# Sign matrices, operand sums and row maxima in a two-layer adjacency kernel: three regroupings

## The chip, the cores and the metric

The kernel runs on one core of one Trainium2 chip. The time is the device time of one execution in microseconds (us), from the first instruction of the program to the last. A core has a matrix engine (TensorE, "PE" in the profile, with its weight loads apart as "PEld"), a vector engine (VectorE, "DVE"), a scalar engine (ScalarE, "ACT"), a general engine (GpSimd, "POOL") and a queue engine (SyncE, "SP"), each with its own list of instructions that it works off in order. Data reach the on-chip memory by DMA transfers, which SyncE, ScalarE or GpSimd issue. The results of TensorE land in PSUM banks, and ScalarE or VectorE takes them from there ("eviction").

## The reference

Two graph layers over 4096 nodes of 512 features, with a dense matrix `adj` of 4096 x 4096. The part that matters, shortened:

```python
# layer 0
bw = sign(w0)
ba = maximum(sign(x), 0)
x  = layernorm(x + relu(adj @ (ba @ bw.T)))
# layer 1
node_att = softmax(x @ node_w, axis=0)
h = x @ edge_w
e = where(adj > 0, h @ h.T, -9e15)
att = node_att * softmax(e, axis=1)
x = layernorm(x + (adj * att) @ (x @ w1) + bias)
```

So layer 0 multiplies a 0/1 matrix by a sign matrix, and then `adj` by the result. Layer 1 needs h, the square matrix `e` with the maximum of each of its rows, and a second product with a 4096 x 4096 matrix.

## The kernel before

The nodes are cut into 32 blocks of 128 (`P`), and into 8 groups of 512 (`W`, `NG = 8`); `BG` = 4 blocks make a group, `KD` = 4 pieces of 128 make up the 512 features, `HG` = 4 pairs of groups (g and g + 4) make up the nodes. TensorE sets the pace nearly everywhere, so the code around it is about what the other engines do and when. Most of the order is found by a scheduler from the data each instruction needs and the order in which the code is written; inside a `tc.manual_schedule(engines=...)` block the named engines take their instructions in written order.

**The sign product and the first two rows of blocks** (lines 165 to 255). `whole(g)` makes the product of the signs for the nodes of group g. It loads the group of x (transposed, 1 MB). Two blocks of nodes are put in one operand: VectorE computes "b > 0, times 2048" into `over` (L186 or L211), and then "a > 0, plus over" into `ba` (L187 or L212). TensorE multiplies `ba` by the weight signs `bw` (L214) into two banks `pw`. Three operations take the two results apart: ScalarE writes `us`, which is rounded so that only the part times 2048 stays (L220), VectorE subtracts it for the first block of `xw` (L222), ScalarE scales it for the second (L223). In group 0, VectorE also makes the weight signs themselves, in two operations for each of four pieces (L204, L206), between those on x. TensorE has nothing to do until the first are there, and is kept busy with products of zeros (`zeros`, L200).

While these products run, two rows of blocks of layer 0's big product (`early`, blocks 0 and 16) are already worked on: `halves(g)` loads four 128 x 128 pieces of `adj` for each of them, and cuts each number into a high part (ScalarE, L236) and the rest (VectorE, L237); `follow(g, ...)` multiplies both parts by `xw` (L246, L247) and adds in the banks `accs`. The loop runs `whole(g + 1)`, `follow(g)`, `halves(g + 1)`. This stage is not in written order: the scheduler mixes the three. Buffers: x and w0 share three (`stream`), the pieces of `adj` share four (`rows`), `hi` and `lo` have two each (`sp`), `ba` has two.

**The other thirty rows of blocks** (to line 383) do the same with 1 MB pieces of `adj` (L363, L365, L373, L374), followed by a layer norm, transposes (L333) and combinations that go out to memory. VectorE and ScalarE are in written order there. `scr` is a buffer of the layer norm. Beside it, `premask` loads parts of `adj`, turns them into masks on VectorE (L281), and stores them through GpSimd's queue (L282).

**h** (lines 386 to 426) is computed by Strassen-Winograd's seven products in place of eight (`seven`). For each pair of groups, four combinations of x are needed as right operands: t1, t2 and t4 on VectorE (L417, L419, L420), t3 on GpSimd (L418). `seven` runs its products in the order 0, 5, 4, 6, 1, 3, 2, each for q = 0 and 1, so there are 14 steps for a pair; t2 serves product 5, t1 product 4, t3 product 6 and t4 product 3. After each step `between_h` may put a `premask` in. The results are added to h on VectorE (L116, L122, L123, L131, L135) or copied by ScalarE (L113, L127).

**`panel(A)`** (from line 765) is called once for each of the eight groups of nodes, in the second half of layer 1. It holds the negated row maxima of the group in `nm`, 128 x 4, and needs them along the free axis and equal on all partitions. For each of four columns TensorE multiplies the column, broadcast to 128 x 128, by the identity (L772); ScalarE copies the bank (L783). The products with `L1065` around it are the attention's.

Of the kernel before, what the change touches and what calls it, by code (L numbers as in the profile page):

```python
# [22 lines left out]
TWO = 2.0**11  # L23
SHIFT = 1.5 * 2.0**34
SPLIT = 6, 4, 3
WARM = 12
# [3 lines left out]
def kernel(  # L30
# [27 lines left out]
    rows = ctx.enter_context(tc.tile_pool(name="rows", bufs=4))  # L58
    small = ctx.enter_context(tc.tile_pool(name="small", bufs=2))
    dram = ctx.enter_context(tc.tile_pool(name="dram", bufs=1, space=bass.MemoryType.DRAM))  # L60
    ps_mm = ctx.enter_context(tc.tile_pool(name="ps_mm", bufs=6, space=bass.MemoryType.PSUM))
# [4 lines left out]
    eps = const.tile([P, 1], F32, name="eps")  # L66
# [92 lines left out]
    with (  # L159
# [14 lines left out]

        us = wp.tile([P, BG // 2, D], F32, name="us", tag="ends")

        def whole(g):

            xt = stream.tile([P, KD, W], F32, name="xt", tag="stream")
            ba = wp.tile([P, KD, W // 2], F32R, name="ba", tag="quarter", bufs=2)  # L180
            pws = [ps_mm.tile([P, D], F32, name="pw", tag="mm") for j in range(BG // 2)]
            order = [(k, j) for j in range(BG // 2) for k in range(KD)]

            def signs(k, over):
                a, b = xt[:, k, : W // 2], xt[:, k, W // 2 :]
                nc.vector.tensor_scalar(over, b, 0.0, TWO, ALU.is_gt, ALU.mult)  # L186
                nc.vector.scalar_tensor_tensor(ba[:, k, :], a, 0.0, over, ALU.is_gt, ALU.add)  # L187

            if g == 0:

                pos = sp.tile([P, KD, D], BF16, name="pos", tag="lo")
                over = sp.tile([P, KD, W // 2], F32, name="over0", tag="hi")
                for k in range(KD):
                    nc.sync.dma_start(w0[:, k, :], w0_t[ts(k, P), :])
                    nc.scalar.dma_start(xt[:, k, :], x_t[ts(k, P), ts(g, W)])
                idle = ps_mm.tile([P, D], F32, name="idle", tag="mm")

                def zeros(n):
                    for _ in range(n):
                        nc.tensor.matmul(idle, warm[:, :P], warm, start=True, stop=True)  # L200

                zeros(WARM)
                for k in range(KD):
                    nc.vector.tensor_scalar(pos[:, k, :], w0[:, k, :], 0.0, None, ALU.is_gt)  # L204
                    signs(k, over[:, k, :])
                    nc.vector.scalar_tensor_tensor(bw[:, k, :], w0[:, k, :], 0.0, pos[:, k, :], ALU.is_lt, ALU.subtract)  # L206
                order = [(k, j) for k in range(KD) for j in range(BG // 2)]
            else:
                nc.sync.dma_start(xt, x_t[:, ts(g, W)].rearrange("(k p) n -> p k n", p=P))
                over = sp.tile([P, KD, W // 2], F32, name="over0", tag="hi")  # L210
                nc.vector.tensor_scalar(over, xt[:, :, W // 2 :], 0.0, TWO, ALU.is_gt, ALU.mult)  # L211
                nc.vector.scalar_tensor_tensor(ba, xt[:, :, : W // 2], 0.0, over, ALU.is_gt, ALU.add)  # L212
            for k, j in order:
                nc.tensor.matmul(pws[j], ba[:, k, ts(j, P)], bw[:, k, :], start=(k == 0), stop=(k == KD - 1))  # L214
                if g == 0 and j == BG // 2 - 1:
                    zeros(3 if k < KD - 1 else 5)
                if k == KD - 1:

                    u = us[:, j, :]
                    nc.scalar.activation(u, pws[j], AF.Identity, bias=shift[:, 0:1])  # L220
                    b = g * BG + j
                    nc.vector.scalar_tensor_tensor(xw[:, b, :], u, SHIFT, pws[j], ALU.subtract, ALU.subtract)  # L222
                    nc.scalar.activation(xw[:, b + BG // 2, :], u, AF.Identity, bias=shift[:, 1:2], scale=-1.0 / TWO)  # L223


        early = [0, HB]
        accs = []

        def halves(g):

            hi = sp.tile([P, QC, P], F32R, name="hi", tag="hi")
            lo = sp.tile([P, QC, P], F32R, name="lo", tag="lo")
            for n, b in enumerate(early):
                a = rows.tile([P, BG, P], F32, name="a0", tag="rows")
                nc.sync.dma_start(a, adj_t[b, :, ts(g, BG), :])
                nc.scalar.copy(hi[:, ts(n, BG), :], a)  # L236
                nc.vector.tensor_sub(lo[:, ts(n, BG), :], a, hi[:, ts(n, BG), :].bitcast(F32))  # L237
            return hi, lo

        def follow(g, hi, lo):  # L240
            if g == 0:
                accs.extend(ps_tr.tile([P, D], F32, name="acc0", tag="tr") for _ in early)
            for n in range(2):
                for c in range(BG):
                    kb = g * BG + c
                    nc.tensor.matmul(accs[n], hi[:, n * BG + c, :], xw[:, kb, :], start=(kb == 0), stop=False)  # L246
                    nc.tensor.matmul(accs[n], lo[:, n * BG + c, :], xw[:, kb, :], start=False, stop=(kb == NB - 1))  # L247

        whole(0)
        parts = halves(0)  # L250
        for g in range(NG):
            if g + 1 < NG:
                whole(g + 1)
            follow(g, *parts)
            if g + 1 < NG:
                parts = halves(g + 1)

        nw_b = wp.tile([P, D], F32, name="nw_b")
        nc.sync.dma_start(nw_b, bass.AP(tensor=node_w.tensor, offset=node_w.offset, ap=[[0, P], [1, D]]))
# [31 lines left out]
        def rest(n, b, xb, acc, before):  # L291

            mv = small.tile([P, 1, nc.vector.BN_AGGR_DIM], F32, name="mv")
            stats = small.tile([P, nc.vector.BN_STATS_DIM], F32, name="stats")
            rstd = small.tile([P, 1], F32, name="rstd")
            scr = wp.tile([P, D], F32, name="scr")
            nc.vector.scalar_tensor_tensor(xb, acc, 0.0, xb, ALU.max, ALU.add)
            nc.vector.bn_stats(stats, xb)
            nc.vector.bn_aggr(mv[:, 0, :], stats)
            yield  # L300
            nc.scalar.activation(rstd, mv[:, :, 1], AF.Sqrt, bias=eps)
            nc.vector.reciprocal(rstd, rstd)
            nc.vector.tensor_scalar(xb, xb, mv[:, 0, 0:1], rstd[:, 0:1], ALU.subtract, ALU.mult)
            nc.vector.tensor_tensor_reduce(
                scr, xb, nw_b, 1.0, 0.0, ALU.mult, ALU.add, accum_out=node_s[:, b : b + 1]
            )
            yield
            nc.vector.tensor_add(scr, xb, bias_b)
            nc.gpsimd.dma_start(x1_d[ts(b, P), :], scr)
            yield  # L310
            if n % 2:
                left(n // 2, before, xb)
            yield
            transpose_rows(b, xb)
# [88 lines left out]
        for _ in range(4):  # L403
            premask(nc.sync, 0, 3)
        count = [0]

        def between_h(q, n):
            count[0] += q is None
            if q is None and count[0] > 6 and count[0] % 5 % 2 == 0:
                premask(nc.sync, 0, 3)  # L410

        for g in range(HG):
            r11, r12 = (x1T[:, :HK, ts(c, W)] for c in (g, g + HG))
            r21, r22 = (x1T[:, HK:, ts(c, W)] for c in (g, g + HG))
            t1, t2 = (sp.tile([P, HK, W], F32, name="t12", tag="hi") for _ in range(2))
            t3, t4 = (sp.tile([P, HK, W], F32, name="t34", tag="lo") for _ in range(2))
            nc.vector.tensor_sub(t1, r12, r11)  # L417
            nc.gpsimd.tensor_sub(t3, r22, r12)  # L418
            nc.vector.tensor_sub(t2, r22, t1)  # L419
            nc.vector.tensor_sub(t4, r21, t2)  # L420
            right_h = r11, r21, r22, t4, t1, t2, t3
            seven(
                lambda m, q: [left_h[m][:, k, ts(q, P)] for k in range(HK)],
                lambda m: [right_h[m][:, k, :] for k in range(HK)],
                [[hT[:, q + f, ts(c, W)] for f in (0, HK) for c in (g, g + HG)] for q in range(2)],
                between_h,
            )
# [337 lines left out]
    def panel(A):  # L765
# [4 lines left out]
        for i in range(BG):  # L770

            nc.tensor.matmul(  # L772
                pt[:, ts(i, P)],
                nm[:, i : i + 1].to_broadcast([P, P]),
                ident,
                start=(i == 0),
                stop=True,
                skip_group_check=i > 0,
            )
        if A % HG:  # L780
# [659 lines left out]
```

## Time and profile before

| | |
|---|---|
| time, three runs | 1941.57 us median (1939.22 to 1943.59) |
| span of the profiled execution | 1940.4 us |
| TensorE busy | 1918.7 us (99%) |
| VectorE busy | 1389.6 us (72%) |
| ScalarE busy | 1022.4 us (53%) |
| GpSimd busy | 299.5 us (15%) |
| moved by DMA | 517.11 MB, mean 267 GB/s |
| weight-sign products L214 | 64, 16.9 us of TensorE |
| early products L246 and L247 | 128, 49.8 us |
| panel products L772 | 64 records, 8.0 us |
| GpSimd's t3, L418 | 4 of 2.34 to 3.20 us |

A line of the timeline is: start in us from the beginning of the span, length in us, engine, source line, operation, output <- inputs by the program's names, partitions x elements and type, count. In brackets is the idle time of the engine just before it, and what ended that idle time. [...] what one costs TensorE is the distance between two starts. A line of the list of waits is: engine and line, what it waited for, us in total, how often, the longest. A line of the windows is: the stretch in us, its length, the busy time of each engine with its number of instructions, the granted TensorE clock, the DMA engines' busy share, GB/s.

### The profile page before, as it was taken

The numbers are of one execution on the slowest core, as the hardware profiler recorded it, in microseconds if no ns is written. First come the engines' busy times: TensorE is split into PE (matmuls) and PEld (weight loads), VectorE is DVE, ScalarE is ACT, GpSimd is POOL, SyncE is SP. The second block draws the span as 40 slices with busy tenths as digits, with TensorE's granted clock in tenths as the row PEclk, the third lists the DMA queues.
The fourth block names the chain that finished last, engine by engine and source line by source line (L and its number), as shares of the span: only waits on it lengthen the run. The fifth ranks groups of instructions, "written<-read, shape, count | busy, mean of one in ns | idle before, by whom it ended". The sixth has DMA issues, their size and how long they took to land.

```text
span 1940.4 us, 20257 instructions
## 1 busy us (share of the span) xinstructions
PE 1918.7 (99%) x6742; PEld 1203.0 (62%) x6742; DVE 1389.6 (72%) x2062; ACT 1022.4 (53%) x1614; POOL 299.5 (15%) x424
## 2 busy tenths in 40 slices
PE   9999999999999999999999999999999999999998
PEld 6888888888644445454555444456666666666655
DVE  7766676676774566567566796687879987798737
ACT  5433333333202567566667566546766576757731
POOL 0122222222341111011112111111111101111100
PEclk9999999999999999999999999999999999999999
DMA  9888888888475478577769998787778787887831
GB/s 311 296 325 310 293 324 308 323 306 293 147 274 213 166 253 320 183 279 254 274 249 336 330 336 296 259 284 248 260 268 290 262 278 254 294 274 265 274 108 44
DMA packets 171751, 517.11 MB, mean 267 GB/s; under 512 B 15872, under 2 KB 41216, under 8 KB 163968
## 3 DMA queue, kind: packets, MB, share of 16 engines
q1 hardware_dynamic: 89472, 226.39, 35.0%
q0 software_dynamic: 66912, 247.49, 34.2%
q10 hardware_dynamic: 15264, 41.95, 5.9%
q8 instruction: 53, 0.87, 0.2%
q14 instruction: 50, 0.41, 0.1%
HBM read 389.94 MB, written 125.83 MB: 266 GB/s over the span
## 4 chain that ended last, share of the span: by engine, by line
PE 76%; DVE 10%; issue 6%; DMA 6%; ACT 1%; POOL 1%; POOLq 0%; DVEq 0%; SPq 0%; ACTq 0%
PE bank L1065 25%; PE seven L702 12%; PE acc L374 11%; PE acc L373 11%; PE pe L633 4%; PE seven L101 4%; PE po L1192 3%; PE pt L603 2%; DMA s_d<-slot 2%; DMA slot<-s_d 2%; DVE lent L835 1%; PE acc L246 1%; PE pw L214 1%; PE pt L333 1%; DVE over L1128 1%
## 5 line engine op out<-in xcount | busy, mean ns | idle before, releaser
L1065 PE MATMUL bank<-lent,lop 128*128 128x512 f32 (+1 forms) x1292 | 424.6, 479 | 0.7 <-issue 0.7
L373 PE MATMUL acc<-xw,hi 128*128 128x512 f32 x960 | 376.4, 392 | 0.0
L374 PE MATMUL acc<-xw,lo 128*128 128x512 f32 x960 | 374.2, 390 | 0.0
L1065 PE MATMUL bank<-slot,lop 128*128 128x512 f32 (+1 forms) x896 | 347.0, 535 | 0.3 <-DVE slot L850 0.3
L1065 PEld LDWEIGHTS bank<-lent,lop 128*128 128x128 f32 x1292 | 245.2, 190 | 155.0 <-issue 133.6
L1065 PEld LDWEIGHTS bank<-slot,lop 128*128 128x128 f32 x896 | 170.0, 190 | 153.4 <-issue 142.3
L363 ACT CAST hi<-at 128x1024 fp32r<-128x1024 f32 x120 | 126.4, 1054 | 203.3 <-PE acc L373 148.4
L365 DVE TENSOR_TENSOR lo<-at,hi 128x1024 fp32r<-128x1024 f32 x120 | 146.9, 1224 | 85.3 <-ACT hi L363 85.3
L374 PEld LDWEIGHTS acc<-xw,lo 128*128 128x128 f32 x960 | 180.3, 188 | 37.0 <-DVE lo L365 0.3
L373 PEld LDWEIGHTS acc<-xw,hi 128*128 128x128 f32 x960 | 180.3, 188 | 36.7
L1074 ACT COPY over<-bank 128x512 f32<-128x512 f32 x200 | 114.9, 581 | 121.3 <-PE bank L1065 109.9
L633 PE MATMUL pe<-hT 128*128 128x512 f32 (+3 forms) x384 | 132.1, 486 | 0.0
L574 ACT ACTIVATE line<-line,nmax_c 128x512 f32<-128x512 f32 x160 | 114.8, 724 | 20.9 <-DVE nmax_c L565 20.8
L565 DVE CUSTOM_DVE_ANT_0 line<-lent,slot 128x512 f32<-128x512 bf16 x144 | 93.1, 689 | 45.2 <-ACT slot L643 22.4
L829 ACT ACTIVATE slot<-slot 128x2048 f32<-128x2048 f32 x40 | 76.5, 1913 | 73.8 <-DMA slot<-in_adj_t_dram 64.7
L823 DVE CUSTOM_DVE_ANT_1 slot<-slot,line 128x2048 f32<-128x2048 f32 x36 | 82.4, 2288 | 32.2 <-DMA slot<-s_d 31.7
L633 PEld LDWEIGHTS pe<-hT 128*128 128x128 f32 x384 | 64.6, 191 | 41.4 <-issue 33.8
L702 PE MATMUL seven<-hT 128*128 128x512 f32 x192 | 89.8, 593 | 0.0
L826 ACT ACTIVATE slot<-slot 128x2048 f32<-128x2048 f32 x36 | 68.9, 1913 | 33.5 <-DVE slot L823 32.5
L1037 ACT COPY bank<-over 128x512 f32<-128x512 f32 x144 | 84.8, 596 | 2.9 <-DVE left L957 0.2
L603 PEld LDWEIGHTS pt<-ident,lent 128*128 128x128 f32 x412 | 51.1, 141 | 55.1 <-issue 40.0
L604 ACT COPY slot<-pt 128x512 f32<-128x512 f32 (+3 forms) x126 | 69.5, 555 | 27.8 <-PE pt L603 24.0
(260 smaller groups left out, 2864.9 us busy)
## 6 DMA issues: line engine op xcount, KB each, us to landing
at<-in_adj_t_dram SPq DMA_DIRECT2D x60, 1024.0 KB, 6.9
slot<-in_adj_t_dram POOLq DMA_DIRECT2D x42, 1024.0 KB, 6.7
lop<-lop_d SPq DMA_DIRECT2D x79, 512.0 KB, 4.7
slot<-s_d POOLq DMA_DIRECT2D x36, 1024.0 KB, 7.5
s_d<-slot POOLq DMA_DIRECT2D x33, 1024.0 KB, 6.9
lent<-s_d POOLq DMA_DIRECT2D x28, 1024.0 KB, 7.9
lop<-lop_d SPq DMA_DIRECT2D x99, 256.0 KB, 4.4
lent<-in_adj_dram SPq DMA_DIRECT2D x48, 512.0 KB, 4.9
```

Source lines behind the costliest of these rows:

```text
L363: nc.scalar.copy(hi, aq)
L365: nc.vector.tensor_sub(lo, aq, hi.bitcast(F32))
L373: nc.tensor.matmul(acc, hi[:, c, :], xw[:, kb, :], start=(kb == 0), stop=False)
L374: nc.tensor.matmul(acc, lo[:, c, :], xw[:, kb, :], start=False, stop=(kb == NB - 1))
L565: nc.vector.tensor_tensor_reduce(line, mask, src, -1.0, HUGE, ALU.add, ALU.min, accum_out=nmax_c[:, b, c : c + 1])
L574: nc.scalar.activation(line, line, AF.Exp, bias=nmax_c[:, b, c : c + 1], scale=-1.0, accum_out=sum_c[:, b, c : c + 1])
L603: nc.tensor.transpose(pt[:, j, :], src[:, ts(j, P)], ident)
L633: nc.tensor.matmul(pe[:, lo * P :], hT[:, k, ts(A * BG + i, P)], hT[:, k, (B * BG + lo) * P : (B + 1) * W], start=(k == 0), stop=(k == KD ...
L702: nc.tensor.matmul(ps, left[m][:, k, q, :], right[m][:, k, :], start=(first and k == 0), stop=(k == KD // 2 - 1), skip_group_check=not first,)
L1037: nc.scalar.copy(self.bank[:, : self.w], self.to())
L1065: nc.tensor.matmul(ps, lop[:, k, :], rop[:, k, :], start=start, stop=(k == K - 1), skip_group_check=True)
L1074: nc.scalar.copy(self.to(), self.bank[:, : self.w])
```

## The change

There are three edits, which don't touch each other.

**The first stage** is rewritten. The weight signs come from ScalarE, one `Sign` with scale -1 for each piece, and a `Sign` on a small tile ahead of them has the function's table loaded early. Of x's group 0, the columns for j = 0 (of both halves) are loaded first, by ScalarE's queue, and those for j = 1 after w0, by SyncE's; the signs of group 0 are made in pieces of 128 columns. `whole` is called for each j, `halves` becomes `split(g, n)` for each of the two early rows, `follow` is called for each n. Loads of x are issued one group further ahead, the signs of x are made one group further ahead, and VectorE, ScalarE and TensorE take all of this in written order. `over` is bf16 and shares a buffer with `scr` in place of one with `hi`.

**h's right combinations** go to VectorE altogether, and those of a pair of groups are made during the products of the pair before, after steps 8, 10 and 13 of its 14.

**`panel`** spreads the row maxima with TensorE's transpose mode: the same operands, with `is_transpose=True`.

```diff
-            if g == 0:
-                pos = sp.tile([P, KD, D], BF16, name="pos", tag="lo")
-                over = sp.tile([P, KD, W // 2], F32, name="over0", tag="hi")
...
-                for k in range(KD):
-                    nc.vector.tensor_scalar(pos[:, k, :], w0[:, k, :], 0.0, None, ALU.is_gt)
-                    signs(k, over[:, k, :])
-                    nc.vector.scalar_tensor_tensor(bw[:, k, :], w0[:, k, :], 0.0, pos[:, k, :], ALU.is_lt, ALU.subtract)
...
+        def signs_x(g):
+            xt = xts.pop(g)
+            ba = wp.tile([P, KD, W // 2], F32R, name="ba", tag="quarter", bufs=2)
+            over = wp.tile([P, KD, W // 2], BF16, name="over0", tag="scr")
...
+            for j in range(BG // 2):
+                for k in range(KD):
+                    if not j:
+                        nc.scalar.activation(bw[:, k, :], w0[:, k, :], AF.Sign, scale=-1.0)
+                    a, b = (xt[:, k, h][:, ts(j, P)] for h in halves)
+                    o = over[:, k, ts(j, P)]
+                    nc.vector.tensor_scalar(o, b, 0.0, TWO, ALU.is_gt, ALU.mult)
+                    nc.vector.scalar_tensor_tensor(ba[:, k, ts(j, P)], a, 0.0, o, ALU.is_gt, ALU.add)
...
+        def whole(g, j):
+            pw = ps_mm.tile([P, D], F32, name="pw", tag="mm")
+            for k in range(KD):
+                nc.tensor.matmul(pw, rights_s[g][:, k, ts(j, P)], bw[:, k, :], start=(k == 0), stop=(k == KD - 1))
+                if g == 0 and (not j or k == KD - 1):
+                    zeros(2 if not j else 4)
...
+        def follow(g, n):
+            hi, lo = split_a[g]
+            for c in (0, 2, 1, 3):
...
+        with tc.manual_schedule(
+            engines={mybir.EngineType.DVE, mybir.EngineType.Activation, mybir.EngineType.PE}
+        ):
+            load_x(0)
...
+            for k in range(KD):
+                nc.sync.dma_start(w0[:, k, :], w0_t[ts(k, P), :])
+                nc.scalar.dma_start(first_x[k][0][:, 0], first_x[k][1][:, 0])
+            for k in range(KD):
+                nc.sync.dma_start(first_x[k][0][:, 1], first_x[k][1][:, 1])
...
+            zeros(WARM)
+            load_a(0, 0)
+            load_x(1)
+            load_a(0, 1)
+            signs_x(0)
+            whole(0, 0)
+            split(0, 0)
+            whole(0, 1)
+            signs_x(1)
+            split(0, 1)
+            for g in range(NG):
+                follow(g, 0)
+                if g + 1 < NG:
+                    for n in range(2):
+                        load_a(g + 1, n)
+                    if g + 2 < NG:
+                        load_x(g + 2)
+                    split(g + 1, 0)
+                    if g:
+                        split(g + 1, 1)
+                        if g + 2 < NG:
+                            signs_x(g + 2)
+                    for j in range(2):
+                        whole(g + 1, j)
+                    if not g:
+                        signs_x(g + 2)
+                        split(g + 1, 1)
+                follow(g, 1)
...
-            nc.gpsimd.tensor_sub(t3, r22, r12)
...
+            nc.vector.tensor_sub(t1, r12, r11)
+            nc.vector.tensor_sub(t2, r22, t1)
+            yield
...
+            nc.vector.tensor_sub(t3, r22, r12)
+            yield
+            nc.vector.tensor_sub(t4, r21, t2)
...
+        ahead_h = deque(p for g in range(1, HG) for p in [rights_h(g)] * 3)
+        for _ in rights_h(0):
+            pass
...
+            if q is None and count[0] % 14 in (8, 10, 13) and ahead_h:
+                next(ahead_h.popleft())
...
                 start=(i == 0),
                 stop=True,
+                is_transpose=True,
                 skip_group_check=i > 0,
```

More of the change, by code (lines that the diff above doesn't have):

```diff
@@ L175 @@
         us = wp.tile([P, BG // 2, D], F32, name="us", tag="ends")
-        def whole(g):
-            xt = stream.tile([P, KD, W], F32, name="xt", tag="stream")
-            ba = wp.tile([P, KD, W // 2], F32R, name="ba", tag="quarter", bufs=2)
[L181 to L187, printed above, removed]
-            if g == 0:
-                pos = sp.tile([P, KD, D], BF16, name="pos", tag="lo")
-                over = sp.tile([P, KD, W // 2], F32, name="over0", tag="hi")
-                for k in range(KD):
[L194 to L202, printed above, removed]
-                for k in range(KD):
-                    nc.vector.tensor_scalar(pos[:, k, :], w0[:, k, :], 0.0, None, ALU.is_gt)
-                    signs(k, over[:, k, :])
-                    nc.vector.scalar_tensor_tensor(bw[:, k, :], w0[:, k, :], 0.0, pos[:, k, :], ALU.is_lt, ALU.subtract)
[L207 to L223, printed above, removed]
@@ L226 @@
[L226 to L238, printed above, removed]
@@ L240, in follow @@
[L240 to L256, printed above, removed]
+        early = [0, HB]
+        accs, xts, rights_s, split_a = [], {}, {}, {}
+        halves = [slice(h * (W // 2), (h + 1) * (W // 2)) for h in range(2)]
+        def load_x(g):
+            xts[g] = stream.tile([P, KD, W], F32, name="xt", tag="stream")
+            if g:
+                nc.sync.dma_start(xts[g], x_t[:, ts(g, W)].rearrange("(k p) n -> p k n", p=P))
@@ new lines, in load_a @@
+        def load_a(g, n):
+            a = rows.tile([P, BG, P], F32, name="a0", tag="rows")
+            nc.sync.dma_start(a, adj_t[early[n], :, ts(g, BG), :])
+            split_a[g, n] = a
+        def signs_x(g):
+            xt = xts.pop(g)
+            ba = wp.tile([P, KD, W // 2], F32R, name="ba", tag="quarter", bufs=2)
+            over = wp.tile([P, KD, W // 2], BF16, name="over0", tag="scr")
+            rights_s[g] = ba
+            if g:
+                nc.vector.tensor_scalar(over, xt[:, :, halves[1]], 0.0, TWO, ALU.is_gt, ALU.mult)
+                nc.vector.scalar_tensor_tensor(ba, xt[:, :, halves[0]], 0.0, over, ALU.is_gt, ALU.add)
+                return
+            for j in range(BG // 2):
+                for k in range(KD):
+                    if not j:
[4 more added lines that the diff above has]
+                    nc.vector.scalar_tensor_tensor(ba[:, k, ts(j, P)], a, 0.0, o, ALU.is_gt, ALU.add)
@@ new lines, in zeros @@
+        def zeros(n):
+            for _ in range(n):
+                nc.tensor.matmul(idle, warm[:, :P], warm, start=True, stop=True)
+        def whole(g, j):
[4 more added lines that the diff above has]
+                    zeros(2 if not j else 4)
+            u = us[:, j, :]
+            nc.scalar.activation(u, pw, AF.Identity, bias=shift[:, 0:1])
+            b = g * BG + j
+            nc.vector.scalar_tensor_tensor(xw[:, b, :], u, SHIFT, pw, ALU.subtract, ALU.subtract)
+            nc.scalar.activation(xw[:, b + BG // 2, :], u, AF.Identity, bias=shift[:, 1:2], scale=-1.0 / TWO)
@@ new lines, in split @@
+        def split(g, n):
+            if not n:
+                hi = sp.tile([P, QC, P], F32R, name="hi", tag="hi")
+                lo = sp.tile([P, QC, P], F32R, name="lo", tag="lo")
+                split_a[g] = hi, lo
+            (hi, lo), a = split_a[g], split_a.pop((g, n))
+            nc.scalar.copy(hi[:, ts(n, BG), :], a)
+            nc.vector.tensor_sub(lo[:, ts(n, BG), :], a, hi[:, ts(n, BG), :].bitcast(F32))
+        def follow(g, n):
+            hi, lo = split_a[g]
+            for c in (0, 2, 1, 3):
+                kb = g * BG + c
+                nc.tensor.matmul(accs[n], hi[:, n * BG + c, :], xw[:, kb, :], start=(kb == 0), stop=False)
+                nc.tensor.matmul(accs[n], lo[:, n * BG + c, :], xw[:, kb, :], start=False, stop=(kb == NB - 1))
@@ new lines @@
+        with tc.manual_schedule(
+            engines={mybir.EngineType.DVE, mybir.EngineType.Activation, mybir.EngineType.PE}
+        ):
+            load_x(0)
+            first_x = [
+                [t.rearrange("p (h j w) -> p j h w", h=2, w=P) for t in (xts[0][:, k, :], x_t[ts(k, P), :W])]
+                for k in range(KD)
+            ]
+            for k in range(KD):
[3 more added lines that the diff above has]
+                nc.sync.dma_start(first_x[k][0][:, 1], first_x[k][1][:, 1])
+            sign = small.tile([P, 1], F32, name="sign")
+            nc.scalar.activation(sign, eps, AF.Sign)
+            idle = ps_mm.tile([P, D], F32, name="idle", tag="mm")
+            accs.extend(ps_tr.tile([P, D], F32, name="acc0", tag="tr") for _ in early)
+            zeros(WARM)
[16 more added lines that the diff above has]
+                    split(g + 1, 0)
+                    if g:
+                        split(g + 1, 1)
[7 more added lines that the diff above has]
+                follow(g, 1)
@@ L295, in rest @@
             rstd = small.tile([P, 1], F32, name="rstd")
-            scr = wp.tile([P, D], F32, name="scr")
+            scr = wp.tile([P, D], F32, name="scr", tag="scr")
             nc.vector.scalar_tensor_tensor(xb, acc, 0.0, xb, ALU.max, ALU.add)
@@ L405, with rights_h @@
         count = [0]
+        rights = {}
+        def rights_h(g):
+            r11, r12 = (x1T[:, :HK, ts(c, W)] for c in (g, g + HG))
+            r21, r22 = (x1T[:, HK:, ts(c, W)] for c in (g, g + HG))
+            t1, t2 = (sp.tile([P, HK, W], F32, name="t12", tag="hi") for _ in range(2))
+            nc.vector.tensor_sub(t1, r12, r11)
+            nc.vector.tensor_sub(t2, r22, t1)
+            yield
+            t3, t4 = (sp.tile([P, HK, W], F32, name="t34", tag="lo") for _ in range(2))
+            nc.vector.tensor_sub(t3, r22, r12)
+            yield
+            nc.vector.tensor_sub(t4, r21, t2)
+            rights[g] = r11, r21, r22, t4, t1, t2, t3
+            yield
+        ahead_h = deque(p for g in range(1, HG) for p in [rights_h(g)] * 3)
+        for _ in rights_h(0):
+            pass
         def between_h(q, n):
             count[0] += q is None
+            if q is None and count[0] % 14 in (8, 10, 13) and ahead_h:
+                next(ahead_h.popleft())
             if q is None and count[0] > 6 and count[0] % 5 % 2 == 0:
@@ L412 @@
         for g in range(HG):
[L413 to L421, printed above, removed]
+            right_h = rights.pop(g)
             seven(
```

## The prediction

> **What bounds the kernel now.** I read the page first (busy shares, granted clock, chain), then the list of what TensorE waited for, then three timelines: the panels, h's third quarter, and the start. From the page:
>
> ```profile
> PE 1918.7 (99%) x6742; PEld 1203.0 (62%) x6742; DVE 1389.6 (72%) x2062; ACT 1022.4 (53%) x1614; POOL 299.5 (15%) x424
> ...
> PEclk9999999999999999999999999999999999999999
> ...
> PE 76%; DVE 10%; issue 6%; DMA 6%; ACT 1%; POOL 1%; POOLq 0%; DVEq 0%; SPq 0%; ACTq 0%
> ```
>
> TensorE is busy 99% at full clock. So time leaves this kernel in only two ways: fewer matmul passes, or fewer of TensorE's own gaps, which are 1940.4 - 1918.7 = 21.7 us in all. Its waits:
>
> ```profile
> PE po L1192 <- DVE xb L1203: 3.8, 6, 1.3
> PE pt L603 <- DVE lent L747: 2.2, 1, 2.2
> PE seven L101 <- DVE hT L122: 1.6, 1, 1.6
> ...
> PE acc L246 <- DVE xw L222: 1.3, 4, 0.6
> ```
>
> (us in total, times, longest). The change touches the third and fourth; the first two lie in stages it leaves alone. Next, two panels of row maxima, seen on TensorE, and one in the earlier stage beside a set of real transposes (start, length, count):
>
> ```profile
> 1231.40 1.95 PE L772 MATMUL bank<-ident,nm 128*128 128x128 f32 x16
> 1233.18 3.17 PE L1065 MATMUL bank<-lent,lop 128*128 128x512 f32 x7
> ...
> 1041.10 0.60 PE L603 MATMUL pt<-ident,lent 128*128 128x128 f32 x4
> 1041.53 1.06 PE L772 MATMUL ptm<-ident,nm 128*128 128x128 f32 x8
> 1042.43 0.81 PE L633 MATMUL pe<-hT 128*128 128x384 f32 x2
> ```
>
> The reader is to count: `panel` writes four matmuls, and the trace has eight records of it; four transposes of the same shape are four records. A written fp32 matmul is two passes here, a transpose is one. In us: 1233.18 - 1231.40 = 1.78 for eight written matmuls, 0.2225 each; 41.53 - 41.10 = 0.43 for four transposes, 0.108 each.
>
> h's third quarter, VectorE, GpSimd and TensorE:
>
> ```profile
> 569.45 0.69 DVE L281 TENSOR_SCALAR more<-more 128x1024 bf16<-128x1024 f32 x1 [4.71 <-DMA more<-in_adj_dram]
> 570.05 1.22 DVE L417 TENSOR_TENSOR t<-x1T 128x1024 f32<-128x1024 f32 x1
> 571.38 3.25 DVE L419 TENSOR_TENSOR t<-x1T,t 128x1024 f32<-128x1024 f32 x1
> ...
> 571.19 2.35 POOL L418 TENSOR_TENSOR t<-x1T 128x1024 f32<-128x1024 f32 x1
> ...
> 575.28 1.12 PE L101 MATMUL seven<-t,we_s 128*128 128x512 f32 x2 [1.64 <-DVE hT L122]
> ```
>
> L419 takes 3.25 us where its three others take 1.22, because GpSimd's L418 runs from 571.19 to 573.54; the eviction L122 is queued behind it on VectorE, and TensorE waits for L122.
>
> The start (TensorE's first product with adj, and the first large x that VectorE uses):
>
> ```profile
> 12.79 0.50 PE L246 MATMUL acc<-xw,hi 128*128 128x512 f32 x1 [0.60 <-DVE xw L222]
> ...
> 13.27 0.70 DVE L211 TENSOR_SCALAR over<-xt 128x1024 f32<-128x1024 f32 x1
> ```
>
> And the windows, 10 to 20 us:
>
> ```profile
> 10.00:20.00 10.00, 9.19 (x39) 6.11 (x38) 8.75 (x14) 7.12 (x12) 0.00 (x0) 1.00 1.05 391
> ```
>
> The DMA engines are full, at 391 GB/s. By the trace's landings, the eight quarters of w0 and x's group 0 land from 4.73 to 8.85 us, adj's first two pieces at 9.51 and 10.46, x's group 1 at 13.17, group 2 at 17.24. Below, this matters more than any engine.
>
> [...] two records of 112 ns against one of 109, so half. [...] 573.54 - 571.38 = 2.16 of blocking plus some 1.1 of work. [...] a load is 1.28 us (the trace has 1283 ns at 2.63)[...].
>
> **Part 1, panels.** Sixteen-record groups: 48 + 16 = 64 records of L772, 32 written matmuls. Each falls from 0.2225 to 0.108-0.109: 32 x 0.114 = 3.6 us of TensorE. All lie on TensorE between other matmuls. The first two panels (0.9 us) come before a stage start where TensorE waits for VectorE (L747), which may swallow some: I book **3.3**, bounds 2.7 and 3.6. The weight load is beside the matmuls.
>
> **Part 2, h.** Removed: four GpSimd subtractions. Added: four VectorE subtractions of 1.22 us. Per quarter of 24 us VectorE then has 10 evictions x 0.6 + 4 x 1.2 + some 8 masks x 0.6 = 15.6 us, so there is room. The pieces go out after steps 8, 10 and 13 of 14, when their buffers' last readers (steps 6, 4 and 8; 12 for t4) are past. An eviction can stand behind t1 and t2 for at most 2.4 us; the bank it frees is next needed a step of 1.7 us or more after that, so TensorE doesn't feel it. Removed [...]: the 1.64 us wait, and about 0.3 us of restart gaps beside it (575.28 to 577.21). The cost: at h's start the third subtraction may delay the last layer norm, for which TensorE's transposes at 512.07 wait; zero if it fills VectorE's 2.4 us of idle at 504.6, 1.1 if not. I take zero to 0.1 and book **1.9**, bounds 0.8 and 2.0.
>
> **Part 3, start.** Before, a k-quarter costs VectorE 1.48 us (L204 from 4.75 to 6.23 to 7.71), four of them 5.9 us. Now weight signs are four ScalarE operations (the 128x512 cast L236 is 0.62), and VectorE has 128x128 pieces, some 0.2 + 0.3 us a pair from the 128x256 rows of 0.29 and 0.42. TensorE's twelve warming matmuls last to 6.37 as before; then four k-steps, spaced by two zeros of 0.22 and w0's landings, end near 9.0, the second half near 10.2. Evictions (0.69 each on ScalarE, then VectorE) and the casts of the first adj piece let `follow(0, 0)` start near 11.1 and end near 13.2. Then TensorE must wait: `whole(1, 0)` needs all of group 1's signs, and x's group 1 can't land before the DMA engines have moved what stands ahead of it. One adj piece of 0.7-0.9 us now comes after it, so it lands at 12.4; against that, x's first group goes in 512-byte pieces. [...] the trace's packets take 27 ns for 512 bytes and 84 for 2048, 29% more per byte, on 1 MB that takes 2.7 us: up to 0.8 later. Landing 12.4 to 13.2, two sign operations of 0.62 and 1.22: `whole(1, 0)` at 14.2 to 15.0, taken 14.6.
>
> From there TensorE has 56 matmuls of `whole` (groups 1-7) and 120 of `follow` (all but the 8 done), 176 x 0.227 = 40.0 us. In the steady order an iteration is 24 x 0.227 = 5.45 us, VectorE's part of it 4.6 (two lo of 0.65, signs 0.6 + 1.2, two xw of 0.65), ScalarE's 3.9, and each result is ready 1 us or more before TensorE asks. Queued behind the signs of group g+2 are the xw evictions of group g+1; once, when group 3's x lands at 21.3-22.1, xw is ready at 23.9-24.7 and TensorE asks at 23.7: 0.6 lost. End: 14.6 + 40.0 + 0.6 = 55.2, where before the next stage begins at 57.19. I book **2.0**, bounds 1.0 and 2.8. The extra table load at the start is hidden before w0's landing at 4.73; the `scr` tag costs nothing, since VectorE alone writes and reads it in order.
>
> **Sum.** 3.3 + 1.9 + 2.0 = 7.2; 1941.6 - 7.2 = 1934.4.
>
> **Rivals.**
> - *Only the panels pay.* The start is bound by x's landings and the gap at 573 comes back elsewhere, for instance behind a mask that waits for its transfer, as the 4.71 us at 569.45 shows. For it: full DMA engines to 19 us. Against: the gaps removed have named causes. Time 1941.6 - 3.3 = 1938.3.
> - *Written order costs (slower).* Each of seven iterations waits because the signs ahead of xw wait for x. With x 1.6 us late each time: 7 x 1.6 = 11.2 lost, 1941.6 + 11.2 - 3.3 - 1.9 - 2.0 = 1945.6. Against: an iteration needs 1.57 MB in 5.45 us, 288 GB/s, where 391 was reached.
> - *More.* A freer GpSimd and earlier masks also shorten gaps in the stages after (from 606 to 1090 us TensorE's starts lie 7.1 us in all beyond their usual spacing): 5 more, 1929.4.
>
> **How the numbers follow.** Forecast 0.62, only panels 0.17, slower 0.10, more 0.11. Faster by over 0.2% means under 1937.7: nearly all of the forecast (0.60), all of "more", a third of "only panels" (0.06): 0.77. Same: the rest, 0.13. Slower 0.10. For the range, 1929.5 cuts half of "more" and 1939.0 the slower case and the upper fringe of "only panels", about 0.2 together; the runs of before spread by 4 us, which is in it.
>
> **What would show it.** Right: L772's successor has 32 records, with eight between neighbours 0.87 us apart; no GpSimd subtraction in h, every t at 1.22, and no wait of 1.6 for L122's successor; the first wide adj product of the next stage near 55.2, TensorE idle once from about 13 to 14.6 with the second x's landing as its cause. Wrong: 64 records still; a wait for xw in every iteration; a new gap near 512; or gaps after 606 that grow by what was won.

## The result: 9 us slower, and where they come from

The changed kernel takes 1950.74 us (median of 5 runs, 1949.13 to 1952.23), the kernel before 1941.57 (1939.22 to 1943.86): a ratio of 1.0041, 95% interval 1.0029 to 1.0053. The forecast was 1934.4, the range ended at 1939.0.

The profile after, from the page (TensorE's row, the granted clock, and two of the costliest groups):

```profile
PE 1925.8 (99%) x6708; PEld 1200.9 (62%) x6708; DVE 1388.4 (71%) x2066; ACT 1023.8 (52%) x1619; POOL 289.1 (15%) x420
...
PEclk9999999999999999999999999999999999999999
...
L403 PE MATMUL acc<-xw,lo 128*128 128x512 f32 x960 | 380.6, 396 | 0.0
L402 PE MATMUL acc<-xw,hi 128*128 128x512 f32 x960 | 380.3, 396 | 0.0
```

TensorE has 34 matmul records fewer (6708 for 6742) and is busy 7.1 us longer. A wait doesn't count as busy, so some products have become longer. L402 and L403 are the L373 and L374 of before, 960 each, the same shapes. The page of before:

```profile
L373 PE MATMUL acc<-xw,hi 128*128 128x512 f32 x960 | 376.4, 392 | 0.0
L374 PE MATMUL acc<-xw,lo 128*128 128x512 f32 x960 | 374.2, 390 | 0.0
```

That is 751 us together before and 761 after. The change does not touch those lines.

What TensorE waited for (us in total, times, longest):

```profile
PE po L1235 <- DVE xb L1246: 3.9, 4, 1.7
PE pw L216 <- DVE ba L198: 3.3, 1, 3.3
PE pt L645 <- DVE lent L789: 2.5, 1, 2.5
PE pt L645 <- ACT lent L685: 2.5, 1, 2.5
```

The wait of h (L122) is gone, as forecast. A new one of 3.3 us stands at the sign products (L216).

The time by stages, from TensorE's first product in each ("wide" are the products of L373 and L374, now L402 and L403, with the 1 MB pieces of adj):

| stage | before | after | difference |
|---|---|---|---|
| start to the first wide adj product | 57.19 | 59.76 | +2.57 |
| wide adj products, to h | 450.31 | 461.63 | +11.32 |
| h | 98.99 | 96.87 | -2.12 |
| the rest, to the last product | 1326.49 | 1325.37 | -1.12 |

So nearly all of the loss lies in a stage that the change does not name. The windows of the wide stage, of before and of after, show that it is no gap: the busy time is the whole stretch in both, with 2042 and 2041 products (the second row of each is h).

```profile
57.19:507.07 449.88, 449.88 (x2042) 372.15 (x2040) 312.30 (x482) 147.43 (x181) 107.71 (x151) 1.00 0.84 303
507.50:606.49 98.99, 97.24 (x230) 42.71 (x229) 66.72 (x98) 12.42 (x22) 32.23 (x37) 1.00 0.53 186
```

```profile
59.76:520.95 461.19, 461.19 (x2041) 372.09 (x2040) 313.40 (x482) 147.07 (x181) 104.99 (x150) 1.00 0.82 295
521.39:618.26 96.87, 96.76 (x230) 42.87 (x229) 66.61 (x101) 12.53 (x22) 24.21 (x34) 1.00 0.56 190
```

The clock is 1.00 in both. Timelines in the middle of the stage, before and then after:

```profile
199.82 0.39 PE L373 MATMUL acc<-xw,hi 128*128 128x512 f32 x1
200.04 0.39 PE L374 MATMUL acc<-xw,lo 128*128 128x512 f32 x1
200.27 0.39 PE L373 MATMUL acc<-xw,hi 128*128 128x512 f32 x1
```

```profile
199.93 0.39 PE L402 MATMUL acc<-xw,hi 128*128 128x512 f32 x1
200.16 0.40 PE L403 MATMUL acc<-xw,lo 128*128 128x512 f32 x1
200.39 0.39 PE L402 MATMUL acc<-xw,hi 128*128 128x512 f32 x1
```

From one start to the next (the shown lengths, 0.39 and 0.40 us, overlap): 0.45 us for a pair before, 0.46 to 0.47 after. Over the whole stage the medians are 227 + 227 ns before, and 231 (after a hi product) + 235 (after a lo product) now, 12 ns more for a pair. 960 pairs x 12 ns = 11.5 us: the whole of the stage's loss, from one end to the other, with nothing beside it to see.

So no gap and no lower clock is to be seen. What does differ for these products in the built program is addresses: where in each partition's memory the tiles lie, in bytes. The small tile `sign` that the early `Sign` writes takes two places of 32 bytes in the pool of small tiles, and every buffer allocated after that pool lies 64 bytes further on in each partition. `xw` is allocated ahead of it and stays at 17472. `lo` and `hi` lay at 209472 and 217664; they lie at 217728 and 209536 now (also in exchanged places, since `pos` and `over0` no longer claim the two tags first; tiles with one tag share buffers). No trace shows these addresses; they follow from the sizes of the tiles allocated ahead.

### The profile page after: what moved, and what is told of

Its sections match the earlier page's. It is cut to its first block, busy times and chain, and to the rows that moved or that the text cites. A ratio compares the mean times of both kernels' runs of the same rounds, so it can differ in the third digit from the quotient of the medians.

```text
span 1950.5 us, 20199 instructions
## 1 busy us (share of the span) xinstructions
PE 1925.8 (99%) x6708; PEld 1200.9 (62%) x6708; DVE 1388.4 (71%) x2066; ACT 1023.8 (52%) x1619; POOL 289.1 (15%) x420
## 4 chain that ended last, share of the span: by engine, by line
PE 84%; DVE 6%; DMA 5%; issue 3%; ACT 1%; POOL 0%; ACTq 0%; POOLq 0%; DVEq 0%
PE bank L1108 31%; PE seven L744 12%; PE acc L403 12%; PE acc L402 11%; PE seven L101 5%; PE pe L675 4%; PE po L1235 4%; PE pt L645 2%; DMA s_d<-slot 2%; DMA slot<-in_adj_t_dram 1%; DVE lent L878 1%; PE acc L238 1%; PE acc L239 1%; PE pt L362 1%; PE pw L216 1%
## 5 line engine op out<-in xcount | busy, mean ns | idle before, releaser
L403 PE MATMUL acc<-xw,lo 128*128 128x512 f32 x960 | 380.6, 396 | 0.0
L402 PE MATMUL acc<-xw,hi 128*128 128x512 f32 x960 | 380.3, 396 | 0.0
L403 PEld LDWEIGHTS acc<-xw,lo 128*128 128x128 f32 x960 | 180.3, 188 | 43.9
L402 PEld LDWEIGHTS acc<-xw,hi 128*128 128x128 f32 x960 | 180.3, 188 | 41.1
```

Of the source, the lines that this page charges most:

```text
L402: nc.tensor.matmul(acc, hi[:, c, :], xw[:, kb, :], start=(kb == 0), stop=False)
L403: nc.tensor.matmul(acc, lo[:, c, :], xw[:, kb, :], start=False, stop=(kb == NB - 1))
```

## The experiments

**Is it the address?** Four kernels on one chip. e1 lets `sign` share a buffer; e3 also restores the places of hi and lo; e2 puts the 64 bytes into the kernel before; e4 is the panel edit alone.

```diff
-            sign = small.tile([P, 1], F32, name="sign")
+            sign = small.tile([P, 1], F32, name="sign", tag="rstd")
```

> The changed kernel with one edit: the small tile that the early Sign writes shares a buffer with rstd, so that no on-chip address after it moves by 64 bytes; hi and lo still stand in exchanged places. Theory address (the 6 ns that each hi and lo product of layer 0 got longer, 227 to 233 ns from start to start, come from where hi and lo lie against xw): products back at 227 ns, the time from the first wide adj product to h back from 461.6 to about 450.3 us, the whole about 11 us below the changed kernel, near 1939. Theory order (the products got longer through the new written order or another stage's work, not through addresses): still 233 ns and 1950. Theory exchange (the exchanged places of hi and lo matter, not the 64 bytes): still 233 ns here, and gone in e3.

1937.35 us, ratio to before 0.9976 (0.9968 to 0.9984). The two groups in its profile:

```profile
L402 PE MATMUL acc<-xw,hi 128*128 128x512 f32 x960 | 376.4, 392 | 0.0
L403 PE MATMUL acc<-xw,lo 128*128 128x512 f32 x960 | 374.2, 390 | 0.0
```

The figures of before to the tenth, 227 ns from start to start, the wide stage 450.34 us. By the medians one tag takes 13 us off the changed kernel, 11.3 of them in the wide stage, and turns slower into faster.

```diff
     node_s = const.tile([P, NB], F32, name="node_s")
+    pad = small.tile([P, 1], F32, name="pad")
+    nc.gpsimd.memset(pad, 0.0)
```

> The kernel before with one edit: a 64-byte unused tile in the pool of small tiles, which moves all buffers after it (x1T, the pieces of adj, hi, lo) by 64 bytes and leaves xw where it was. Theory address: hi and lo products go from 227 to about 233 ns, layer 0's wide stage from 450.3 to about 461 us, the whole from 1941 to about 1952. Theory order and theory exchange: no change, 1941.

1952.37 us, ratio 1.0053 (1.0036 to 1.0070), 231 and 235 ns, wide stage 461.61 us. An unused tile alone makes the kernel before as slow as the changed one:

```profile
L376 PE MATMUL acc<-xw,lo 128*128 128x512 f32 x960 | 380.6, 396 | 0.0
L375 PE MATMUL acc<-xw,hi 128*128 128x512 f32 x960 | 380.3, 396 | 0.0
```

```diff
-                hi = sp.tile([P, QC, P], F32R, name="hi", tag="hi")
                 lo = sp.tile([P, QC, P], F32R, name="lo", tag="lo")
+                hi = sp.tile([P, QC, P], F32R, name="hi", tag="hi")
```

> As e1, and lo is allocated ahead of hi, so that both lie at the addresses of the kernel before. Theory address: same as e1, near 1939, 227 ns. Theory exchange: 227 ns only here. Theory order: 233 ns, 1950.

1938.62 us, ratio 0.9985 (0.9974 to 0.9995), 227 ns. As e1: the exchanged places play no part, and theory order and theory exchange have both fallen.

**Whose address, and against what?** e7 moves hi and lo alone (with the operands of h, which use the same buffers); e8 moves everything, xw too.

```diff
+        pad = sp.tile([P, 1], F32, name="pad")             # e7: pool of hi and lo
...
+    pad = const.tile([P, 16], F32, name="pad")             # e8: ahead of xw
```

> The kernel before with a 64-byte unused tile in the pool of hi and lo alone: only hi, lo and h's operands move, x1T, adj's pieces and xw stay. Theory operands (the distance of the two things TensorE reads, xw and hi or lo, sets the 6 ns): 231 and 235 ns as in e2, time near 1952. Theory writers (where adj's pieces or x1T lie, which DMA and other engines write): 227 ns, time as before.

> The kernel before with 64 unused bytes ahead of xw: everything moves by 64, xw too. Theory relative (only the distance between xw and hi or lo counts): 227 ns, time as before, near 1941. Theory absolute, hi and lo (where hi and lo lie counts): 231 and 235 ns, near 1952. Theory absolute, xw (each of the two costs if it is at one of the two places): between them or above.

e7: 1954.08 us, ratio 1.0056 (1.0038 to 1.0074). e8: 1942.76 us, 0.9993 (0.9985 to 1.0002). In both, hi and lo lie at the very same addresses; only xw differs. e7's two groups, and then e8's:

```profile
L376 PE MATMUL acc<-xw,lo 128*128 128x512 f32 x960 | 380.8, 397 | 0.0
L375 PE MATMUL acc<-xw,hi 128*128 128x512 f32 x960 | 380.1, 396 | 0.0
```

```profile
L375 PE MATMUL acc<-xw,hi 128*128 128x512 f32 x960 | 376.6, 392 | 0.0
L376 PE MATMUL acc<-xw,lo 128*128 128x512 f32 x960 | 374.2, 390 | 0.0
```

So it is the distance between what TensorE streams (xw) and what it loads as weights (hi, lo): of what keeps its old distance from them in e8 and not in e7, these products read xw alone. Where hi and lo lie by themselves doesn't matter. Nor does where adj's pieces lie: e2 moved them together with hi and lo, e7 left them, and both are slow.

**Which distance?** The kernel before with hi and lo moved by 32, 128, 256 and 512 bytes.

```diff
+        pad = sp.tile([P, 1], F32, name="pad", bufs=1)     # e10: 32 bytes
...
+        pad = sp.tile([P, 16], F32, name="pad")            # e11: 128; e13: 32 columns, 256; e14: 64 columns, 512
```

> The kernel before with hi and lo moved by 32 bytes alone, so that they lie 32 and not 0 bytes (mod 128) from xw. Theory distance of 64: only a place in the other half of 128 bytes costs, so 227 ns and 1941. Rival (any offset from xw other than a multiple of 128 costs): between 229 and 236 ns, 1945 to 1954.

> The kernel before with hi and lo moved by 128 bytes alone. Theory distance, with a period of 128 bytes: 227 ns, time as before, near 1941. Rival (any move away from the addresses of before costs, or a longer period): 231 and 235 ns, near 1952.

> The kernel before with hi and lo moved by 256 bytes alone. Theory period 256 (the distance from hi and lo to xw must be a multiple of 256 bytes): 227 ns, near 1942. Theory period 512 (a multiple of 512, one row of a 128-column operand, as in the kernel before): 231 to 237 ns, near 1954. Theory any move: 231 to 237 ns.

> The kernel before with hi and lo moved by 512 bytes alone. Theories period 256 and period 512: 227 ns, near 1942. Theory any move, or a longer period: 231 to 237 ns, near 1954.

| moved by | hi and lo to xw, mod 256 | ns after a hi, after a lo product | wide stage | time | ratio to before |
|---|---|---|---|---|---|
| 0 (before) | 0 | 227, 227 | 450.31 | 1941.57 | 1 |
| 32 (e10) | 32 | 235, 232 | 461.40 | 1955.49 | 1.0067 (1.0044 to 1.0090) |
| 64 (e7) | 64 | 231, 236 | 461.62 | 1954.08 | 1.0056 (1.0038 to 1.0074) |
| 128 (e11) | 128 | 237, 229 | 461.19 | 1954.37 | 1.0061 (1.0038 to 1.0085) |
| 256 (e13) | 0 | 227, 227 | 450.32 | 1942.03 | 1.0000 (0.9990 to 1.0010) |
| 512 (e14) | 0 | 227, 227 | 450.32 | 1941.63 | 0.9995 (0.9985 to 1.0005) |

My first guess was that only a place in the other half of 128 bytes costs. It fell in e10, where 32 bytes cost as much, and in e11, where 128 did (two executions each). A move by 256 or 512 costs nothing that shows. e11's groups show how the loss is shared out differently while the sum stays (383.7 + 377.0 = 760.7, in e7 760.9):

```profile
L375 PE MATMUL acc<-xw,hi 128*128 128x512 f32 x960 | 383.7, 400 | 0.0
L376 PE MATMUL acc<-xw,lo 128*128 128x512 f32 x960 | 377.0, 393 | 0.0
```

**The start.** The other loss, +2.57 us. The changed kernel's timelines of SyncE's issues, of VectorE and of TensorE:

```profile
3.90 2.38 SPq L253 DMA_DIRECT2D xt<-in_x_t_dram  x4
6.98 0.34 SPq L188 DMA_DIRECT2D a<-in_adj_t_dram  x1
8.06 0.37 SPq L184 DMA_DIRECT2D xt<-in_x_t_dram  x1
```

```profile
15.24 0.69 DVE L197 TENSOR_SCALAR over<-xt 128x1024 bf16<-128x1024 f32 x1 [2.68 <-DMA xt<-in_x_t_dram]
15.96 1.23 DVE L198 SCALAR_TENSOR_TENSOR ba<-xt,over 128x1024 fp32r<-128x1024 f32 x1
```

```profile
13.51 0.39 PE L239 MATMUL acc<-xw,lo 128*128 128x512 f32 x1
17.25 0.72 PE L216 MATMUL pw<-bw,ba 128*128 128x512 f32 x2 [3.35 <-DVE ba L198]
```

x's group 1 (the issue at 8.06) lands at 15.14; before, it was issued at 5.82 and landed at 13.17. The first issue is at 3.90, right after w0's first piece has landed (3.89), and the one at 8.06 comes right after x's fourth early piece has (8.04). In the trace the ninth transfer to the 16th each wait on a semaphore that one of the first eight used, so that of these no more than eight are under way at once. Group 1 was the 11th and is the 14th now, with four late pieces of x and one adj piece fewer ahead of it. The DMA engines are not full all the while: from 9 to 11 us they have less to do than before (share and GB/s are the last two figures; before, then after):

```profile
9.00:11.00 2.00, 2.00 (x10) 0.81 (x8) 2.00 (x6) 1.14 (x2) 0.00 (x0) 1.00 1.03 357
```

```profile
9.00:11.00 2.00, 1.95 (x8) 0.92 (x8) 1.90 (x8) 1.70 (x3) 0.28 (x1) 1.00 0.79 232
```

And then the windows of the changed kernel (the clock is the third figure from the end):

```profile
14.00:16.00 2.00, 0.00 (x0) 0.00 (x0) 0.73 (x2) 0.16 (x1) 0.00 (x0) 1.00 1.01 371
16.00:18.00 2.00, 0.76 (x3) 0.67 (x4) 2.00 (x3) 1.08 (x2) 0.00 (x0) 1.00 1.05 408
18.00:20.00 2.00, 2.00 (x7) 1.52 (x6) 1.08 (x2) 1.41 (x2) 0.00 (x0) 0.57 0.90 298
20.00:22.00 2.00, 2.00 (x7) 1.56 (x6) 1.07 (x2) 1.75 (x3) 0.00 (x0) 0.58 0.99 328
```

After 3.35 us of idleness TensorE goes on at 17.25, and from 18.28 to 21.68 the granted clock is 0.50 (0.57 and 0.58 in the last two windows): eight products there are 0.42 us apart and not 0.23, another 1.6 us. The addresses cost in this stage too: after 26 us its hi and lo products are 233 ns apart in the median, in e1 227, which over the 120 that follow the wait is an estimated 0.7 us.

```diff
             for k in range(KD):
-                nc.sync.dma_start(first_x[k][0][:, 1], first_x[k][1][:, 1])
+            for h in halves:                                # e5, on top of e1
+                late = slice(h.start + P, h.stop)
+                nc.sync.dma_start(xts[0][:, :, late], x_t[:, late].rearrange("(k p) n -> p k n", p=P))
```

> As e1, and the second half of x's first group is loaded by two transfers in place of four, so that x's group 1 is the 12th transfer and no longer the 14th. Theory in-flight (a ninth transfer is issued only when one of eight has landed, so that two transfers more or less move the issue of x's group 1): issued near 6.1 us and not at 8.0, landed near 13.5 and not at 15.6, TensorE's wait ahead of group 1's sign products 4.0 us in e1, below 2.5 here, no slow products after it, the wide stage begins near 56 and not 61.4, the whole 4 to 5 us below e1. Rival (bytes: the DMA engines can't bring group 1 earlier whatever is issued): landing stays near 15.6, the whole as e1.

```diff
-                nc.scalar.dma_start(first_x[k][0][:, 0], first_x[k][1][:, 0])
+                nc.scalar.dma_start(xts[0][:, k, :], x_t[ts(k, P), :W])     # e6, on top of e1
...
-            for k in range(KD):
-                nc.sync.dma_start(first_x[k][0][:, 1], first_x[k][1][:, 1])
```

> As e1, without the halving: x's first group is loaded in four whole pieces on ScalarE's queue as in the kernel before, no later pieces. Theory in-flight: x's group 1 is issued near 5.8 us and lands near 12.5; the first product of layer 0 starts some 0.5 us later than in e1, but TensorE's wait ahead of group 1 falls to about 1 us; wide stage near 55 us, the whole 5 to 6 us below e1 and at or below e5. Rival (bytes or written order): the wait stays at 3 to 4 us, the wide stage begins near 60.

e5: 1936.87 us, ratio 0.9964 (0.9951 to 0.9978). e6: 1935.61 us, 0.9963 (0.9949 to 0.9976). e5's timelines of SyncE and of TensorE, and its windows:

```profile
5.73 0.43 SPq L184 DMA_DIRECT2D xt<-in_x_t_dram  x1
```

```profile
15.35 0.39 PE L239 MATMUL acc<-xw,lo 128*128 128x512 f32 x1
16.38 0.98 PE L216 MATMUL pw<-bw,ba 128*128 128x512 f32 x3 [0.64 <-DVE ba L198]
```

```profile
18.00:20.00 2.00, 2.00 (x11) 1.62 (x10) 1.01 (x2) 1.94 (x4) 0.00 (x0) 1.00 0.90 238
```

Issued at 5.73 and landed at 13.74 (e6: 4.81 and 12.68), a wait of 0.64 in place of 3.35, the clock at 1.00: the number of transfers sets when group 1 comes, and the bytes alone don't (e5 moves the same bytes in the same 512-byte packets as e1, where group 1 landed at 15.62). But the expected 56 and 55 us for the first wide product were not reached, nor the 4 to 6 us below e1 in the whole: by the ratios it is 2.3 and 2.5. The first wide product comes at 58.26 and 57.15. The changed kernel, e3 and e1, which share one first stage, have 59.76, 60.15 and 61.39; the kernels with the old first stage and xw at its right distance have 56.94 to 57.93. So even mended, the rewritten stage starts the next one no earlier than the old stage does.

**The two other edits alone.**

```diff
                 stop=True,
+                is_transpose=True,
                 skip_group_check=i > 0,
```

> The kernel before with the panel edit alone (is_transpose). Prediction's step: 32 records of the panels in place of 64, 3.6 us of TensorE less, time 2.7 to 3.6 us below before. Rival (swallowed by TensorE's waits later): 0 to 2 us below before, with longer waits at 1080 us and in the output products.

1937.07 us, ratio 0.9975 (0.9966 to 0.9983), 4.9 us less (3.3 to 6.6), 32 records in place of 64. The shorter products account for 3.6; if the gain is really larger, nothing here says why. Two panels in the changed kernel's timeline:

```profile
1244.43 1.04 PE L814 MATMUL bank<-ident,nm 128*128 128x128 f32 x8
1245.31 1.88 PE L1108 MATMUL bank<-lent,lop 128*128 128x512 f32 x4
```

0.88 us where before has 1.78, as forecast (0.87). From h's end to the last product, the seven profiles with the edit average 1324.4 us (1322.6 to 1325.9), the nine without it 1327.5 (1325.8 to 1329.8): 3.1 us.

```diff
-            nc.gpsimd.tensor_sub(t3, r22, r12)
+            nc.vector.tensor_sub(t3, r22, r12)              # and the rest of the h edit
```

> The kernel before with the h edit alone. Prediction's step: no GpSimd subtraction, every VectorE subtraction of h near 1.22 us, no wait of 1.6 us at the third quarter, h 96.9 us where before has 99.0, time 1.9 us below before (0.8 to 2.0). Rival (the gap turns up behind a mask or at h's start): h stays at 98 or more, time as before.

> The kernel before with the h edit and the panel edit, its first stage untouched. If the rewritten first stage brings nothing even with its addresses and transfers mended, this is as fast as e6: 1.9 + 3.3 = 5.2 us below before, near 1937. If the rewritten stage brings the 2.0 us predicted, e6 is 2 us faster than this.

e9: 1941.65 us, ratio 0.9995 (0.9986 to 1.0004). h is 96.87 us, as expected, and its wait is gone from the list, but other waits are longer (the first row was 3.8 in before), and the first wide product comes at 57.93:

```profile
PE po L1205 <- DVE xb L1216: 5.9, 8, 1.7
PE acc L246 <- DVE xw L222: 1.9, 4, 1.2
```

So the stage gains 2.1 us and the whole can't be told from no change; 1.9 us less is still inside the interval. e12: 1937.43 us, 0.9976 (0.9962 to 0.9990), as the sum of the two edits had it. e6, which has the mended first stage besides, is 2.5 us faster by the two ratios, but their intervals overlap; in the profiles its wide stage begins 0.5 us earlier (57.15 against 57.68). So the booked 2.0 us of the start isn't shown, and the times alone don't rule it out.

The wait in h also comes and goes without the edit. h takes 98.4 to 99.0 us in six of the nine profiles of kernels with GpSimd's t3, and 96.87 in the three others (e2, e7, e14); in the seven kernels with the edit it is always 96.87 or 96.88. In e2, VectorE is first, and GpSimd is the one that is held up; VectorE's and GpSimd's timelines:

```profile
581.52 1.22 DVE L421 TENSOR_TENSOR t<-x1T,t 128x1024 f32<-128x1024 f32 x1
```

```profile
581.68 3.29 POOL L420 TENSOR_TENSOR t<-x1T 128x1024 f32<-128x1024 f32 x1 [0.36 <-PE seven L103]
```

So it is the third quarter of before with the engines exchanged: the one that started first took the time it also takes elsewhere in h (before, GpSimd's L418 2.35 us; in e2, VectorE's L421 1.22), and the other took longer (before, VectorE's L419 3.25; in e2, GpSimd's L420 3.29).

## Why the prediction was wrong, step by step

**What failed first: the sum had three terms.** "3.3 + 1.9 + 2.0" takes every other stage as unchanged. It had no term for addresses, and the tile `sign` was never costed at all. That missing term is +11.3 us in the wide stage, and it alone turns the sign of the result: with it taken out (e1) the change makes the kernel 0.24% faster, where 0.37% was forecast.

**Part 3, start (booked -2.0, measured +2.57).** The step that failed is "landing 12.4 to 13.2 ... `whole(1, 0)` at 14.2 to 15.0". The landing was 15.14 and the product came at 17.25. I had added up bytes and 512-byte packets, and had not counted transfers. A wait of 1.4 us was forecast where it was 3.35, and after it the granted clock was 0.50 for 3.4 us (1.6 more); the addresses add an estimated 0.7. The steps ahead of it held: `follow(0, 0)` was forecast for 11.1 and began at 11.64. The 0.6 us wait for group 3's xw is not in the list of waits. With the transfers mended, the profiles have the term at about zero (57.15 to 58.26 against 57.19) and not at -2.0: `follow(0, 0)` then begins at 13.1 to 13.5, because x's or w0's last pieces land up to 1.7 us later than in the changed kernel, and in written order the signs of group 1 stand behind the evictions of group 0 on VectorE. This last reason was read from the traces and not tried by itself.

**Part 2, h (booked -1.9, measured -2.12 in the stage, a little beyond the bound of 2.0).** The cause was right: with nothing of h on GpSimd, all 16 subtractions take 1.22 us on VectorE. And h's start cost nothing, as I had taken it. But the wait is a matter of which engine comes first, and it isn't there in every kernel; in the whole time its gain was not resolved (e9).

**Part 1, panels (booked -3.3).** Right: 32 records, 0.88 us for two panels, 3.1 us over all profiles. In the one profile of the changed kernel only 1.1 us of it is left after h; the waits at `pt` are 2.2 us longer there (2.5 + 2.5, before 2.2 + 0.6), which makes up the difference.

**The slower rival** had the direction for the wrong reason. Nothing waits for xw in every iteration.

**The best version.** e6, the changed kernel with `sign` in `rstd`'s buffer and x's first group loaded whole, has the lowest ratio, 0.9963 of before, where the changed kernel has 1.0041. e1, e3, e4, e5 and e12 are faster than before too, and their intervals overlap with e6's.

## What to carry to other kernels

When a stage that the change doesn't touch gets longer with no gap and at the same clock, compare the distance between two starts of the same product, and then the addresses in the built program. A new small tile moved everything behind it by 64 bytes here, which cost 11.3 us in the wide stage; give such a tile a buffer that exists already, or pad to the old distance. And before a load is cut into more pieces, count the transfers ahead of the one that the next step needs, not the bytes alone.

## What the runs showed of the hardware that was not expected

- The wide stage's 128x512 products of fp32r operands took 227 ns from start to start with hi and lo moved by 0, 256 and 512 bytes, which leaves the weights a multiple of 256 bytes from the streamed xw in the partition, and 233 ns on average with moves of 32, 64 and 128: 2.6% more. With xw moved along by 64 (e8) it was 227 again. The fp32 passes of h took 429 ns both before and after, though the t operands moved with hi and lo. What does it inside the chip was not tried, nor was a move of xw alone.
- A written fp32 product is two records here (before, 112 ns each at 128 columns), a transpose one of 109 (after).
- One idle stretch of 3.35 us at the start was followed by a granted clock of 0.50 from 18.28 to 21.68 us, which cost 1.6 us more. In e5 and e6, where it was 0.64 and 0.61 us, the granted clock was 1.00 in every window from 12 to 22 us.
